# Reordering the opening of a graph-network kernel: who issues the loads, in which order, and which engine copies the first pair

## Chip, cores, metric

One core of one Trainium2 chip. The metric is the device time of one launch in microseconds (us).

## The reference, cut to what matters

For each of 64 graphs of 256 nodes and 256 channels: layer norm and ReLU; then a gated update fed by a convolution branch and a message branch.

```python
h  = relu(bn(conv1d(xc, conv1_w, pad=0)))            # 256 x 256, one tap
h  = bn(conv1d(h, conv2_w, pad=8))                   # 256 x 256 x 17 taps
x_conv = relu(h + xc).T
A   = exp(-dist) * mask;  msg = relu(x @ w_msg.T + b_msg)
x_nmp = A @ msg
# ... GRU gates from [x_conv, x_nmp] and x; the result is added to the input
```

All is float32. The 17-tap convolution is done as a short transform along the nodes with 47 products per block, so the filters must first be transformed too: this is work that only the start of the launch has.

## The kernel before

The kernel takes the graphs as 32 pairs, in eight blocks of four pairs. Before the first block it must (1) load x, normalize it, turn it with TensorE and run conv1 on four pairs; (2) load the filter taps (4.46 MB as `taps`, 119 rows of 7 input channels times 17 taps, loaded in three *thirds* for each half of the channels, `dc`), multiply them with three constant matrices (`points`, one for each *pass*), 57 *filter steps* of two matmuls each (four instructions in the trace), copy each result out on ScalarE and store it to DRAM (`filt`, 12.3 MB); (3) read `filt` back one kind at a time (`wb`) for the products.

```python
norm(0)                                  # pair 0 on VectorE
...
w_c1 = const.tile([P, DC, D], FP)
nc.scalar.dma_start(out=w_c1, ...)
s1, h1_shift = fold_bn(bn_vecs(bn1, "bn1", nc.scalar), "bn1")   # strided: one element per packet
...
def load_taps(dc, a, b, eng):
    eng.dma_start(out=taps[:, a:b, dc, :],
                  in_=c2_wT[dc * P + a * KG:dc * P + b * KG].rearrange("(g k) t o -> (k t) g o", k=KG))
...                                       # three loads of points, on nc.scalar
for h in range(3):
    for dc in range(DC):
        load_taps(dc, h * (NG - 1) // 3, (h + 1) * (NG - 1) // 3, nc.scalar if dc else nc.sync)
...
def transpose_h(i):                       # copies on ScalarE; x of pairs 2 and 3 loaded by ScalarE's queue
    ...
            nc.scalar.activation(HT[i][:, dc, :], p, AF.Relu)
    if i + 2 < B // G:
        load_x(i + 2, nc.scalar if i < 2 else nc.sync)
...
steps = [(m, g) for m in range(len(PASSES)) for g in range(NG)]
transpose_h(0); norm(1)
for j in range(PB):                       # PB = 4 pairs, four filter steps each
    if j > 0:
        transpose_h(j)
    if 0 < j < PB - 1:
        norm(j + 1)
    conv1(j)
    run(split_steps(j))
    for m, n in steps[j * 4:(j + 1) * 4]:
        filters(m, n, nc.sync)
forward()                                 # the block's transform, on VectorE
for j, (m, n) in enumerate(steps[PB * 4:]):          # the other 41 filter steps
    filters(m, n, nc.gpsimd if j % 2 else nc.sync)
```

`filters` writes PSUM with TensorE, copies on ScalarE into one of six staging tiles `fo`, and stores that. The queues run in order: ScalarE issues its loads among its own instructions. In the traces PE is TensorE and PEld its weight loads, DVE is VectorE, ACT ScalarE, POOL GpSimd and SP SyncE; a q behind a name (ACTq) marks the issue of a transfer.

Of the kernel before, what the change touches and what calls it, by code (L numbers as in the profile page):

```python
# [13 lines left out]
FP = mybir.dt.float32  # L14
U16 = mybir.dt.uint16
AF = mybir.ActivationFunctionType
ALU = mybir.AluOpType
# [284 lines left out]
def kernel(  # L302
# [26 lines left out]
    nc = tc.nc  # L329
    P = 128  # L330
    B, N, D = x.shape
    G = 2
    GB = 8
    PB = GB // G
    NB = B // GB
    DC = D // P
    MC = N // P
    W = G * N
    TAPS = c2_wT.shape[1]
    SE = se_wT.shape[1]  # L340
# [3 lines left out]
    NW = N // L  # L344
# [4 lines left out]
    const = ctx.enter_context(tc.tile_pool(name="const", bufs=1))  # L349
    work = ctx.enter_context(tc.tile_pool(name="work", bufs=1))  # L350
    stage_ctx = ExitStack()
    stage = stage_ctx.enter_context(tc.tile_pool(name="stage", bufs=1))
    psum = ctx.enter_context(tc.tile_pool(name="psum", bufs=1, space=bass.MemoryType.PSUM))
# [21 lines left out]
    def load_rows(t, src, i, eng):  # L375
        for g in range(G):
            eng.dma_start(out=row_tile(t, g), in_=rows(src, G * i + g))

    def load_x(i, eng=nc.sync):
        X[i] = work.tile([P, G * MC, D], FP, name="x", bufs=2)  # L380
        load_rows(X[i], x, i, eng)
# [23 lines left out]
    def load_adj(i, eng=nc.gpsimd):  # L405
        if i >= B // G:
            return
        if i < BY_DMA:
            ADJ[i] = work.tile([P, G * MC, N], FP, name="adj")
            load_rows(ADJ[i], adj, i, eng)  # L410
            return
        ADJH[i] = late.tile([P, 2 * MC, W], U16, name="adjh")
        for q in range(2 * MC):
            eng.dma_start(out=ADJH[i][:, q], in_=ADJD[i][:, q])
# [24 lines left out]
    ident = const.tile([P, P], FP)  # L439
    make_identity(nc, ident)  # L440
    neg_half = const.tile([P, G * MC], FP)
    nc.gpsimd.memset(neg_half, -0.5)

    pace = Pace()

    def mm(p, w, v, columns, **kw):
# [3 lines left out]
    def transpose(p, v):  # L450
        nc.tensor.transpose(p, v, ident)  # L451
        pace.tensor(P / 2)

    PSUM, ACT = 0.2, 0.9

    HT, MSG, E, AT, XNM = {}, {}, {}, {}, {}


    def norm_steps(i):
# [26 lines left out]
    def run(steps):  # L486
        for n, call in steps:
            pace.vector(n)
            call()

    def norm(i):
        a, b = norm_steps(i)
        run(a)
        pace.vector(0, pace.dve + 1.4)
        run(b)

    norm(0)

    def vec(src, name, eng=nc.gpsimd):
        k = src.shape[0] // P  # L500
        t = const.tile([P, k], FP, name=name)
        eng.dma_start(out=t, in_=src.rearrange("(k p) -> p k", p=P))
        return t

    def bn_vecs(params, name, eng=nc.gpsimd):
        return [vec(a, f"{name}_{s}", eng) for a, s in zip(params, "gbmv")]

    def fold_bn(params, name, factor=1.0):
        g, b, m, v = params
        scale = const.tile([P, DC], FP, name=f"{name}_scale")  # L510
        shift = const.tile([P, DC], FP, name=f"{name}_shift")
        nc.vector.tensor_scalar(scale, v, BN_EPS, None, ALU.add)
        nc.gpsimd.tensor_tensor(scale, scale, neg_half[:, :DC], ALU.pow)
        nc.vector.tensor_mul(scale, scale, g)
        nc.vector.tensor_mul(shift, m, scale)
        nc.vector.tensor_sub(shift, b, shift)
        if factor != 1.0:
            nc.vector.tensor_scalar(scale, scale, factor, None, ALU.mult)
        return scale, shift

    w_c1 = const.tile([P, DC, D], FP)
    nc.scalar.dma_start(out=w_c1, in_=c1_wT.rearrange("(k p) o -> p k o", p=P))
    s1, h1_shift = fold_bn(bn_vecs(bn1, "bn1", nc.scalar), "bn1")


    KG = P // TAPS
    NG = -(-P // KG)
    taps = stage.tile([KG * TAPS, NG, DC, D], FP, name="taps")

    def load_taps(dc, a, b, eng):  # L530
        eng.dma_start(out=taps[:, a:b, dc, :],
                      in_=c2_wT[dc * P + a * KG:dc * P + b * KG].rearrange("(g k) t o -> (k t) g o", k=KG))

    PASSES = [range(0, 6), range(6, 12), range(12, 16)]
    points = []
    for n, bins in enumerate(PASSES):
        f = filter_points(bins, TAPS)
        m = np.zeros((KG, TAPS, KG, f.shape[1]), np.float32)
        for k in range(KG):
            m[k, :, k] = f  # L540
        t = stage.tile([KG * TAPS, KG * f.shape[1]], FP, name=f"points{n}")
        nc.scalar.dma_start(out=t, in_=nc.inline_tensor(m.reshape(KG * TAPS, -1), name=f"points{n}").ap())
        points.append(t)
    for h in range(3):
        for dc in range(DC):
            load_taps(dc, h * (NG - 1) // 3, (h + 1) * (NG - 1) // 3, nc.scalar if dc else nc.sync)
    for dc in range(DC):
        last = c2_wT[dc * P + (NG - 1) * KG:(dc + 1) * P]
        nc.sync.dma_start(out=taps[:last.shape[0] * TAPS, NG - 1, dc, :], in_=last.rearrange("k t o -> (k t) o"))


    Z = const.tile([P, 1 + MC, G * MC, Q], FP, name="z")
# [5 lines left out]
    h1 = const.tile([P, G * DC, L, NW + 2], FP, name="h1")  # L558
# [3 lines left out]
    PT, Sv, T = (Slots(t, GB * DC, L // 4, NW) for t in (PTt, Svt, Tt))  # L562
    Yu = V

    def aux():
        return psum.tile([P, W], FP, name="aux", bufs=3)

    def acc():
        return psum.tile([P, W], FP, name="acc", bufs=5)


    def transpose_h(i):
        if i >= B // G:
            return
        HT[i] = work.tile([P, DC, W], FP, name="hT", bufs=6)
        for dc in range(DC):
            p = aux()
            for j in range(G * MC):
                transpose(chunk(p, j // MC, j % MC), X[i][:, j, dc * P:(dc + 1) * P])
            nc.scalar.activation(HT[i][:, dc, :], p, AF.Relu)  # L580
        if i + 2 < B // G:
            load_x(i + 2, nc.scalar if i < 2 else nc.sync)



    def conv1(i):
        if i >= B // G:
            return
        for o in range(DC):
            p = acc()  # L590
            for k in range(DC):
                mm(p, w_c1[:, k, o * P:(o + 1) * P], HT[i][:, k, :], W, start=(k == 0), stop=(k == DC - 1))
            nc.scalar.activation(h1.rearrange("p (g o) s b -> p o g s b", o=DC)[:, o, :, :, 1:1 + NW],  # L593
                                 p.rearrange("p (g s b) -> p g s b", g=G, b=NW),
                                 AF.Relu, bias=h1_shift[:, o:o + 1], scale=s1[:, o:o + 1])
        pace.vector(0, pace.pe + ACT)

    def split_steps(i):
# [15 lines left out]
    def filters(m, g, eng):  # L614

        kinds = filt[m].shape[1]
        size = min(KG, P - g * KG)
        p = acc()
        for dc in range(DC):
            mm(p[:size * kinds, dc * D:(dc + 1) * D], points[m][:size * TAPS, :size * kinds],  # L620
               taps[:size * TAPS, g, dc, :], D, start=True, stop=True)
        t = stage.tile([P, W], FP, name="fo", bufs=6)
        nc.scalar.copy(t[:size * kinds], p[:size * kinds])
        eng.dma_start(
            out=filt[m][g * KG:g * KG + size].rearrange("k t c o -> (k t) (c o)"), in_=t[:size * kinds])
# [219 lines left out]

    w_ih = const.tile([P, 2 * DC, 3 * D], FP)
    w_hh = const.tile([P, DC, 3 * D], FP)
    steps = [(m, g) for m in range(len(PASSES)) for g in range(NG)]
    transpose_h(0)
    norm(1)  # L850

    w_msg = const.tile([P, DC, D + SE], FP)
    nc.sync.dma_start(out=w_msg[:, :, :D], in_=msg_wT.rearrange("(k p) o -> p k o", p=P))
    nc.gpsimd.dma_start(out=w_msg[:, :, D:], in_=se_wT.rearrange("(k p) s -> p k s", p=P))
    b_msg = const.tile([P, D + SE], FP)
    for t, v in ((b_msg[:, :D], msg_b), (b_msg[:, D:], se_b)):
        nc.gpsimd.dma_start(out=t, in_=bass.AP(tensor=v.tensor, offset=v.offset, ap=[[0, P], [1, v.shape[0]]]))
    load_adj(0, nc.sync)
    bn2 = bn_vecs(bn2, "bn2")
    b_ih, b_hh = vec(ih_b, "b_ih"), vec(hh_b, "b_hh")  # L860
    for j in range(PB):
        if j > 0:
            transpose_h(j)
        if 0 < j < PB - 1:
            norm(j + 1)
        conv1(j)
        run(split_steps(j))
        for m, n in steps[j * 4:(j + 1) * 4]:
            filters(m, n, nc.sync)
    s2, h2_shift = fold_bn(bn2, "bn2", 1.0 / L)  # L870
    b_rz = const.tile([P, 2 * DC], FP)
    nc.vector.tensor_add(b_rz, b_ih[:, :2 * DC], b_hh[:, :2 * DC])
# [2 lines left out]
    forward()  # L875
    for j, (m, n) in enumerate(steps[PB * 4:]):
        filters(m, n, nc.gpsimd if j % 2 else nc.sync)
        if j + PB * 4 == 2 * NG - 10:
            for n in range(3):
                for kind in range(3):  # L880
                    load_kind(0, n, kind)
# [5 lines left out]
    for b in range(NB):  # L887
        i = b * PB
# [41 lines left out]
        stats, scale = norm_steps(nxt + 1)  # L930
# [33 lines left out]
        stats, scale = norm_steps(nxt + 2)  # L964
# [11 lines left out]
        stats, scale = norm_steps(nxt + 3)  # L976
# [70 lines left out]
```

## Time and profile before

| | before |
|---|---|
| time, median of 3 runs | 1899.43 us (1896.17 to 1899.59) |
| TensorE busy in the profiled run | 1827.6 of 1895.5 us |
| conv1 of pair 0 starts | 27.48 us |
| 16th filter step ends | 68.6 us |
| first message product (all filter steps done) | 111.51 us |
| first filter product | 115.12 us |

The last three are milestones read from TensorE's rows in the timeline. The message product stands right behind the last filter step in TensorE's order, so its start is the length of the opening. To read the rows of the waits: who waited, for whom, total us, times, longest. A row of the timeline has start, duration, engine, line, operation, out<-in, shapes and count, and in brackets the idle time before it and what ended that. A row of the windows has the window and its length, the busy time of PE, PEld, DVE, ACT and POOL, each with the number of instructions, then the granted clock, the DMA share and GB/s. The DMA share adds up the times of packets, which can overlap, so it can pass 1. The rows that the prediction rests on are shown in it.

### The profile page before, as it was taken

The page shows a single profiled execution, that of the slowest core. Times are in us where ns is not written, and L with a number is a line of the kernel's source. Part 1 is how long each engine was busy: PE and PEld are TensorE (multiplying, and loading weights), DVE is VectorE, ACT ScalarE, POOL GpSimd, SP SyncE. Part 2 cuts the span into 40 slices and gives each one's busy share as a digit, 9 for nine tenths or more (in the row PEclk, how much of TensorE's full clock was granted, in tenths as well). Part 3 has the DMA queues.
Part 4 walks back from the last instruction along what each step waited for, and adds up shares of the span by engine and source line. Part 5 has one row for each costly group of instructions (what it writes and reads, how often), then busy time and mean ns, then how long its engine had stood idle before and what let it go on. Part 6 is the DMA issues. An engine that isn't in the chain of part 4 may idle for free.

```text
span 1895.5 us, 21978 instructions
## 1 busy us (share of the span) xinstructions
PE 1827.6 (96%) x7708; PEld 1136.6 (60%) x7708; DVE 1393.1 (73%) x2667; ACT 639.4 (34%) x1338; POOL 208.2 (11%) x324
## 2 busy tenths in 40 slices
PE   3999999999999999999999999999999999999997
PEld 2677445865549554694458755495546944586543
DVE  2888648996499945998379964999559983798522
ACT  1534322243313443244232433134432352224311
POOL 2110110110111010111101001101101111010000
PEclk9999999999999999999999999999999999999999
DMA  5777331762318431482316613274313923073010
GB/s 161 253 237 216 91 87 36 195 176 57 85 48 244 107 93 52 112 239 56 89 34 191 182 54 82 54 237 114 90 55 106 239 62 78 23 186 104 2 43 23
DMA packets 180215, 217.63 MB, mean 115 GB/s; under 512 B 86146, under 2 KB 105858, under 8 KB 180105
## 3 DMA queue, kind: packets, MB, share of 16 engines
q1 hardware_dynamic: 145228, 156.03, 28.8%
q0 software_dynamic: 30432, 56.53, 12.7%
q10 hardware_dynamic: 4445, 3.67, 0.6%
q8 instruction: 61, 1.00, 0.2%
q14 instruction: 49, 0.40, 0.1%
HBM read 156.54 MB, written 44.30 MB: 106 GB/s over the span
## 4 chain that ended last, share of the span: by engine, by line
PE 82%; DVE 8%; DMA 4%; issue 3%; ACT 2%; POOL 1%; POOLq 0%; DVEq 0%; ACTq 0%
PE acc L447 70%; PE aux L447 8%; PE aux L451 3%; DMA taps<-in_c_wT_dram 1%; DVE Yv L59 1%; PE aux L736 1%; DVE e L743 1%; DVE Yv L62 1%; DMA x<-in_x_dram 1%; DVE T L65 1%; DVE Yv L65 1%; DVE V L65 1%; DMA wb<-filt 1%; DVE msg L708 1%; DVE T L62 0%
## 5 line engine op out<-in xcount | busy, mean ns | idle before, releaser
L447 PE MATMUL acc<-hT,w_hh 128*128 128x512 f32 x768 | 353.9, 597 | 1.9 <-ACT h L593 1.9
L447 PE MATMUL acc<-xnm,w_ih 128*128 128x512 f32 x768 | 353.0, 594 | 0.0
L447 PE MATMUL acc<-Yv,w_ih 128*128 128x512 f32 x768 | 341.1, 593 | 9.5 <-ACT Yv L696 9.5
L447 PEld LDWEIGHTS acc<-Yv,w_ih 128*128 128x128 f32 x768 | 145.2, 190 | 196.3 <-issue 177.2
L447 PEld LDWEIGHTS acc<-xnm,w_ih 128*128 128x128 f32 x768 | 145.6, 190 | 183.3 <-issue 181.3
L447 PEld LDWEIGHTS acc<-hT,w_hh 128*128 128x128 f32 x768 | 143.5, 191 | 169.5 <-issue 161.4
L797 ACT ACTIVATE tr<-acc,b_rz 128x512 f32<-128x512 f32 x64 | 44.0, 687 | 540.8 <-PE acc L447 540.8
L799 DVE SCALAR_TENSOR_TENSOR gn<-tr,gn 128x512 f32<-128x512 f32 x64 | 44.2, 690 | 207.7 <-ACT tr L797 207.7
L825 POOL DMA_DIRECT2D out_dram<-y x64 | 39.2, 617 | 886.4 <-DVE y L824 885.0
L447 PE MATMUL acc<-hT,w_c 128*128 128x512 f32 x256 | 117.9, 604 | 15.2 <-ACT hT L580 15.2
L447 PE MATMUL acc<-U,wb 128*128 128x128 f32 x1024 | 124.6, 276 | 0.5 <-DMA wb<-filt 0.5
L447 PE MATMUL acc<-V,wb 128*128 128x128 f32 x1024 | 124.8, 275 | 0.0
L447 PEld LDWEIGHTS acc<-U,wb 128*128 128x128 f32 x1024 | 120.5, 192 | 4.3 <-DVE Yv L59 2.3
L59 DVE SCALAR_TENSOR_TENSOR V<-T,V 128x256 f32<-128x256 f32 (+2 forms) x224 | 121.5, 606 | 0.3
L447 PEld LDWEIGHTS acc<-V,wb 128*128 128x128 f32 x1024 | 119.5, 192 | 0.0
L447 PE MATMUL aux<-e,msg 128*128 128x256 f32 x464 | 104.9, 379 | 0.0
L447 PEld LDWEIGHTS aux<-e,msg 128*128 128x128 f32 x464 | 86.1, 190 | 11.4 <-issue 1.0
L476 POOL TENSOR_TENSOR rstd<-rstd,neg_half 128x4 f32<-128x4 f32 x32 | 36.3, 1135 | 502.0 <-DVE rstd L475 502.0
L824 DVE TENSOR_TENSOR y<-aux,y 128x512 f32<-128x512 f32 x64 | 41.1, 683 | 68.4 <-PE aux L451 68.4
L447 PE MATMUL aux<-w_msg,hT 128*128 128x259 f32 x384 | 89.4, 381 | 0.0
L65 DVE TENSOR_TENSOR V<-h 128x512 f32<-128x512 f32 x64 | 43.8, 684 | 60.8 <-ACT h L593 60.8
L447 PEld LDWEIGHTS acc<-hT,w_c 128*128 128x128 f32 x256 | 49.2, 194 | 65.2 <-issue 45.1
(141 smaller groups left out, 2727.6 us busy)
## 6 DMA issues: line engine op xcount, KB each, us to landing
wb<-filt SPq DMA_DIRECT2D x376, 256.0 KB
y<-in_x_dram POOLq DMA_DIRECT2D x64, 256.0 KB, 5.7
out_dram<-y POOLq DMA_DIRECT2D x64, 256.0 KB, 5.1
x<-in_x_dram SPq DMA_DIRECT2D x60, 256.0 KB
halves_d<-halves SPq DMA_DIRECT2D x116, 128.0 KB
adjh<-halves_d POOLq DMA_DIRECT2D x116, 128.0 KB, 5.5
filt<-fo SPq DMA_DIRECT2D x26, 252.0 KB
filt<-fo POOLq DMA_DIRECT2D x10, 252.0 KB, 5.6
```

Of the source, the lines that this page charges most:

```text
L59: return self.step(out, lambda: self.v.scalar_tensor_tensor(out, x, s, y, op0=ALU.mult, op1=ALU.add))
L62: return self.step(out, lambda: self.v.tensor_add(out, x, y))
L65: return self.step(out, lambda: self.v.tensor_sub(out, x, y))
L447: nc.tensor.matmul(p, w, v, **kw)
L451: nc.tensor.transpose(p, v, ident)
L476: nc.gpsimd.tensor_tensor(t["rstd"], t["rstd"], neg_half, ALU.pow)
L708: nc.vector.tensor_add(MSG[i][:, g, c, :], p[:, :D + SE], b_msg)
L736: nc.tensor.matmul(p[:, :N], ZT[rows_q, :P], ZT[rows_q, P:], start=True, stop=True)
L797: nc.scalar.activation(tr, pr, AF.Tanh, bias=b_rz[:, dc:dc + 1], scale=0.5)
L799: nc.vector.scalar_tensor_tensor(gn, tr, 1.0, gn, op0=ALU.add, op1=ALU.mult)
L824: nc.vector.tensor_add(row_tile(Y[i], g), p, row_tile(Y[i], g))
L825: nc.gpsimd.dma_start(out=rows(out, G * i + g), in_=row_tile(Y[i], g))
```

## The change

Its intent: let nothing that TensorE needs early stand behind something that is needed late. Small vectors come as rows of 128 elements and are turned by TensorE; ScalarE issues only what is needed first, the rest goes to SyncE in order of need; filter steps of all three passes run on the first third of the taps; pair 0's two copies are VectorE's. Cut to its core:

```diff
+    load_vectors("bn1", bn1, nc.scalar)
+    w_c1 = const.tile([P, DC, D], FP)
+    nc.scalar.dma_start(out=w_c1, in_=c1_wT.rearrange("(k p) o -> p k o", p=P))
+    load_taps(0, *THIRDS[0], nc.sync)
+    load_taps(1, *THIRDS[0], nc.scalar)
...
+    bn1 = columns("bn1")                  # TensorE transpose, VectorE copy
+    nc.scalar.activation(const.tile([P, 1], FP, name="unused"), neg_half[:, :1], AF.Relu)
...                                        # the points stay here, on nc.scalar
-    for h in range(3):
-        for dc in range(DC):
-            load_taps(dc, h * (NG - 1) // 3, (h + 1) * (NG - 1) // 3, nc.scalar if dc else nc.sync)
+    load_taps(1, *THIRDS[1], nc.scalar)
...
-            nc.scalar.activation(HT[i][:, dc, :], p, AF.Relu)
+            if i == 0:
+                nc.vector.tensor_scalar(HT[i][:, dc, :], p, 0.0, None, ALU.max)
+            else:
+                nc.scalar.activation(HT[i][:, dc, :], p, AF.Relu)
...                                        # the same for h1 in conv1
-            load_x(i + 2, nc.scalar if i < 2 else nc.sync)
+            load_x(i + 2)
...
-    steps = [(m, g) for m in range(len(PASSES)) for g in range(NG)]
+    FIRST = THIRDS[0][1]
+    steps = [(m, g) for g in range(FIRST) for m in range(len(PASSES))]
+    steps += [(m, g) for m in range(len(PASSES)) for g in range(FIRST, NG)]
     transpose_h(0)
+    load_taps(0, *THIRDS[1], nc.sync)
     norm(1)
     for j in range(PB):
...
+        if j == 1:
+            for dc in range(DC):
+                load_taps(dc, *THIRDS[2], nc.sync)
+            for dc in range(DC):
+                load_last_taps(dc, nc.sync)
...                                        # w_msg, its bias, adj(0), bn2 rows: at j == 2
-        if j + PB * 4 == 2 * NG - 10:     # filt is first read after this step
+        if (m, n) == (1, NG - 4):
```

## The prediction

> **What bounds the kernel now.** I read the page first: its busy line, then its slices.
>
> ```profile
> span 1895.5 us, 21978 instructions
> ...
> PE 1827.6 (96%) x7708; PEld 1136.6 (60%) x7708; DVE 1393.1 (73%) x2667; ACT 639.4 (34%) x1338; POOL 208.2 (11%) x324
> ...
> PE   3999999999999999999999999999999999999997
> ```
>
> TensorE is busy 96% of the span; the idle share is 1895.5 − 1827.6 = 67.9 us. One slice is 47.4 us, and the first is the only one that stands at 3 tenths. The change touches nothing but the start, so its prize is TensorE's idle time there. Next I asked the view of waits for the first 150 us:
>
> ```profile
> ACT L580 <- DMA taps<-in_c_wT_dram: 25.5, 1, 25.5
> ...
> ACT fo L623 <- DMA filt<-fo: 18.3, 16, 4.1
> ...
> PE acc L447 <- ACT hT L580: 15.2, 3, 14.6
> ...
> PE aux L451 <- DVE x L479: 10.6, 1, 10.6
> ...
> PE acc L447 <- ACT fo L623: 5.7, 4, 3.2
> ...
> PE acc L447 <- ACT h L593: 4.0, 1, 4.0
> ```
>
> The four rows of PE sum to 15.2 + 10.6 + 5.7 + 4.0 = 35.5 us: this is all that the start can give. The first row names the cause of the largest: ScalarE did nothing for 25.5 us, and what ended it was a tap transfer. The timeline shows how:
>
> ```profile
> 9.02 16.48 ACTq L531 DMA_DIRECT2D taps<-in_c_wT_dram  x3
> ...
> 10.57 2.30 PE L451 MATMUL aux<-ident,x 128*128 128x128 f32 x8 [10.57 <-DVE x L479]
> ...
> 25.53 1.28 ACT L580 ACT_TABLE_LOAD   x1 [25.53 <-DMA taps<-in_c_wT_dram]
> 26.82 1.08 ACT L580 ACTIVATE hT<-aux 128x512 f32<-128x512 f32 x2
> ...
> 27.48 5.38 PE L447 MATMUL acc<-hT,w_c 128*128 128x512 f32 x8 [14.61 <-ACT hT L580]
> ...
> 35.84 2.64 ACTq L377 DMA_DIRECT2D x<-in_x_dram  x2
> ...
> 38.61 1.45 ACT L593 ACTIVATE h<-acc,bn_shift,bn_scale 128x512 f32<-128x512 f32 x2 [10.70 <-DMA taps<-in_c_wT_dram]
> ```
>
> The first pair's transposes end at 10.57 + 2.30 = 12.87, but the copy that follows stands behind ScalarE's own issue of three tap loads (9.02 + 16.48 = 25.5) and a table load, so TensorE stands until 27.48. Then ScalarE is held again: its x loads for pair 2 are issued only at 35.84, and the copy of conv1 runs at 38.61, which is the 4.0 us row. The last view is the table of windows for the filter transform's second half:
>
> ```profile
> 76.00:90.00 14.00, 14.00 (x65) 11.07 (x65) 13.97 (x28) 7.09 (x13) 3.73 (x7) 1.00 0.90 270
> 90.00:101.00 11.00, 5.19 (x21) 2.36 (x20) 10.90 (x13) 3.07 (x6) 1.05 (x2) 1.00 0.81 306
> 101.00:112.00 11.00, 11.00 (x50) 7.07 (x51) 4.81 (x8) 7.56 (x16) 3.69 (x7) 1.00 0.67 192
> ```
>
> The last two columns are the DMA share and GB/s. From 76 to 101 us the transfers are nearly full and TensorE, which runs up to 11 filter steps ahead (6 staging and 5 PSUM buffers), stands 5.8 us. The timeline ends the filter steps on TensorE at 111.5 us; there the first message product starts. From there on the order of work is that of before.
>
> **What the skill says.** (1) "DMA: Bandwidth & Descriptors", section "Why a DMA increments its semaphore by 16 and not by 1": a transfer runs on the largest number of engines up to 16 that divides the slowest dimension. A tap load has 7 × 17 = 119 rows, so 7 engines; a filter store of 126 rows gets 14; x with 128 rows gets 16. The trace agrees: with taps in flight (12 to 28 us) the DMA share is 0.56 at 156 GB/s, little above 7/16 = 0.44, whichever of the two queues they use. (2) The same page, "Issuing engines are not separate DMA queues": all queues use the same 16 engines, so moving loads from ScalarE to SyncE frees ScalarE and adds no bandwidth. The 156 GB/s on two queues agree. (3) The same page, "Rules for kernel authors": a load without contiguous last dimension becomes one descriptor per element. The DMA view of the first 36 us counts 1824 packets under 512 B in 5.58 MB. (4) "ScalarE: Activation LUTs", section "What ACT_TABLE_LOAD costs", has 1283 ns; the trace has 1.28 us.
>
> **The change, part by part.**
>
> *First pair on VectorE.* hT and h1 of pair 0 leave ScalarE. VectorE adds 2 copies of 128x512 (about 0.68 us each, from the trace's 128x512 VectorE rows) and 2 × 2 operations for h1 (2.6 us together at most). x arrives as before, so the transposes end near 13. VectorE runs the bn1 fold first (0.16 us operations around one 0.70 us POOL power: to about 13.3), so the copies end near 14.7 and conv1 starts at about 14.0 instead of 27.5: **13.5 us earlier**. VectorE then runs norm(1) (1.4 + 0.36 + 0.17 + a 1.2 us wait + 1.54 = 4.7 us) to 19.4, then h1 to 22, then four splits (2.5 us) to 24.5. The PSUM copy is thus no longer at 38.6, and the **4.0 us** stall goes.
>
> *Tap order and queues.* The first filter steps need only thirds 0 of both halves and the points. Two loads of 714 KB at about 156 GB/s are 9.2 us; beside x (1 MB on all 16 engines, 3 us on each) they land near 16 to 17, and conv1 keeps TensorE till about 19. So the first four filter steps are not held. Interleaving the three passes makes 18 steps possible on these thirds, where before any step past the sixth needed a later third.
>
> *Per pair,* TensorE then has 8 transposes (1.0), 8 conv1 matmuls (3.6 with the wait for hT about 4.6) and four filter steps (4 × 0.88 = 3.5): 9 us, the pace that the trace shows from 51 to 60. Pairs 1 to 3 start at 23.5 and end at 23.5 + 3 × 9 = 50.5. At half clock for some us (the 36 to 44 window had 0.61) and for one hold I add 2.5: 53. Before, this point was at 68.2 (64.5 + 4 × 0.9). **15 us earlier.**
>
> *The hold.* SyncE now issues third 2 and the last taps (1.5 MB, 9.5 us on 7 engines) ahead of the second pair's filter stores. I put those stores' landing at 44 us: on each low engine 131 KB of x, 16 of w_c1, 620 of taps and 125 of eight filter steps are about 0.9 MB, at 156/7 = 22 GB/s 41 us from 3 us on. With six staging buffers, the copies of steps 11 and 12 wait a few us; part of it is in the 2.5.
>
> *The other 41 filter steps* took 111.5 − 68.2 = 43.3 us before (41 × 0.87 = 35.7 of matmul and 5.8 of stalls on stores). Now they hold 8.4 MB of stores instead of 8.2, the same prefetch of 2.3 MB of filters (issued after step 40, not 28, among smaller stores). Fewer other loads remain, but all is crowded into less time. I take 38 to 43: filters end at 91 to 96, against 111.5.
>
> *Vectors as rows.* 14 strided loads of 4-byte elements (256 or 768 each) become rows of 512 B; two TensorE transposes and two small VectorE copies are added, under 1 us. ScalarE's issue of four of them (2.4 us) lay beside the x load and was hidden; POOL's (17.8 to 22.3) too. Worth about 0 to 0.5 us by itself.
>
> *Early table load:* 1.28 us, no longer ahead of the first copy, already counted in the 13.5.
>
> **Sum.** 111.5 − 93.5 = 18, plus half a us of small things, less half for the bn2 transposes: a gain of 18. No wait downstream takes it back in my view: odd FFT work on VectorE, which ended near 94.4, moves forward with pair 3's splits (68.4 to about 51).
>
> **Rivals.** (a) *The DMA becomes the bound.* By 118 us before, the DMA views' windows sum to 0.34 + 6.62 + 7.03 + 6.97 + 2.91 = 23.9 MB. At the 290 GB/s that 76 to 100 us reached, that is 82 us, but taps hold 7 engines for 28 us. Against it: shares stood at 0.4 to 0.6 until 44. For it: 76 to 101. If it rules, filters end at 100 and the gain is 11: 1888. (b) *The wait moves to SyncE:* stores behind third 2 stop ScalarE and so the hT copies of pairs 2 and 3. Then 3 to 6 us are lost: 1885 to 1888. (c) *VectorE becomes the start's bound:* if norm(1) ahead of h1 delays split(0) and norm(2), each pair waits; it has 14 us of work in pair 0 and under 6 in each later pair of 9, so I expect no more than 2 us. (d) *Stores hide everything better than thought,* and TensorE stands only for the first 13 us and 2 more: gain 35.5 − 15 = 20 to 22, 1878.
>
> **Range and chances.** 1899.4 − 18 = **1881.4 us**. Rival (d) and a little less half clock give the low end 1875; (a) with (b) the high end 1890. Two per cent are 38 us, more than the 35.5 that stand idle, so faster by 2% is nearly ruled out; slower would need the whole gain and 38 us more to be lost.
>
> **What would show it right or wrong.** In the timeline after: conv1's first matmul at about 14 (not 27); no ACT row released by taps; pair 3's last filter step near 53; the first message product near 93; PE rows of the waits summing to some 17 us in the first 120, with "DVE x" at about 10 among them. From the message product to the end both traces should take the same 1784 us within 2. Wrong if "ACT fo <- DMA filt" rises well over 18.3 with PE behind it, if the first filter steps wait for taps, or if the products start by waiting for filters not yet loaded.

## The result, and the profile after

The changed kernel took 1896.05 us (1893.43 to 1900.28, 4 runs) beside 1899.51 for the kernel before (now also 4 runs). The ratio is 0.9986, 95% interval 0.9963 to 1.0009: the same. Ratios here are the mean time of one kernel's runs over that of the other's of the same rounds, so not quite the ratio of the quoted medians. The prediction had 1881.4 and a range of 1875 to 1890. Of the 18 us that were predicted, 3 to 4 came by the medians, and the interval does not tell even these from nothing.

The profiled execution of the changed kernel was its slowest run, so ends of spans are not compared below; milestones are. The page of the kernel after:

```profile
span 1898.5 us, 21985 instructions
...
PE 1836.8 (97%) x7710; PEld 1141.9 (60%) x7710; DVE 1398.1 (74%) x2675; ACT 637.4 (34%) x1335; POOL 206.4 (11%) x324
...
PE   6899899999999999999999999999999999999997
```

The first slice went from 3 to 6 tenths, so the start did improve; but the second has lost its nine. TensorE's busy time *rose* by 9.2 us, for two more small matmuls of some 0.24 us each. The waits of the kernel after, in its first 150 us:

```profile
ACT fo L646 <- DMA filt<-fo: 21.3, 14, 5.2
...
PE acc L479 <- ACT hT L599: 5.5, 3, 4.9
PE acc L479 <- ACT fo L646: 5.0, 5, 1.7
PE acc L479 <- DMA points<-points: 4.7, 2, 4.0
```

The 15.2 us wait for ScalarE's hT copy has shrunk to 5.5 and the row "ACT L580 <- DMA taps" is gone, as meant. A new row has come, 4.7 us for the points, and ScalarE's wait for filter stores has grown from 18.3 to 21.3. The timeline of the kernel after tells where each stands:

```profile
13.43 5.58 PE L479 MATMUL acc<-hT,w_c 128*128 128x512 f32 x8 [0.92 <-DVE hT L597]
...
23.05 1.10 PE L479 MATMUL acc<-taps,points 119*126 119x256 f32 x4 [4.04 <-DMA points<-points]
...
34.15 3.80 SPq L451 DMA_DIRECT2D taps<-in_c_wT_dram  x2
...
37.99 6.07 SPq L456 DMA_DIRECT2D taps<-in_c_wT_dram  x2
...
44.16 1.92 SPq L647 DMA_DIRECT2D filt<-fo  x4
...
51.40 1.16 ACT L646 COPY fo<-acc 126x512 f32<-126x512 f32 x2 [5.21 <-DMA filt<-fo]
...
53.10 6.22 PE L479 MATMUL acc<-hT,w_c 128*128 128x512 f32 x8 [4.93 <-ACT hT L599]
...
107.29 5.55 PE L479 MATMUL aux<-w_msg,hT 128*128 128x259 f32 x12
...
113.61 1.05 PE L479 MATMUL acc<-Sv,wb 128*128 128x128 f32 x8
```

conv1 starts 14.0 us earlier. Then TensorE waits for the points; then the second pair's filter stores are issued only at 44.16, after the last taps, ScalarE finds no free staging tile for 5.21 us, and pair 3's conv1 stands. The message product comes 4.2 us earlier than before, the first filter product 1.5 us. The windows of the kernel after:

```profile
12.00:28.00 16.00, 10.40 (x23) 5.24 (x22) 12.09 (x37) 1.17 (x2) 3.73 (x7) 0.88 0.52 163
20.00:30.00 10.00, 6.31 (x16) 4.43 (x17) 6.44 (x19) 1.75 (x3) 1.01 (x1) 0.70 0.56 190
50.00:60.00 10.00, 6.89 (x12) 3.32 (x13) 0.00 (x0) 3.48 (x6) 0.00 (x0) 0.66 0.67 232
101.00:112.00 11.00, 9.28 (x23) 5.37 (x22) 1.88 (x5) 3.67 (x7) 2.07 (x4) 0.57 0.43 139
```

Each of the two waits is followed by a stretch of low granted clock, and so is the ragged end of the filter steps; in the last window before, the clock was 1.00. This accounts for most of the added busy time: up to the first filter product the mean clock was 0.89 against 0.97 before, and TensorE was busy for 87.5 against 79.4 us. The Trainium skill, page "TensorE: Matmul & The Clock Gate", section "HAM oscillation — how this bites in real kernels", describes it: after an idle gap of more than about 3.4 us the clock falls to half. The traces agree for the two waits: gaps of 4.04 and 4.93 us, then 0.70 and 0.66. They do not show that the gap must be that long: no gap at the ragged end is over 1.73 us, and in after_taps16 below the clock was 0.50 from 43.2 to 46.6 us, behind a gap of 1.74 us. Part of each of the two waits is paid a second time, as slower work after it.

Two causes are then possible. **Theory H**: the gain went into these holds and their clock; take the holds away and it comes back. **Rival B**: the transfers set the end of the filter steps, and waits on TensorE before it are only where the slack shows. In B's special form it is the taps, which by the skill's divisor rule run on 7 of 16 engines: the DMA share from 12 to 28 us is 0.52 at 163 GB/s, much as before the change (0.56 at 156).

### The profile page after: what moved, and what is told of

The parts are those of the page before. It is cut to its first block, busy times and chain, and to the rows that moved or that the text cites. A ratio compares the mean times of both kernels' runs of the same rounds, so it can differ in the third digit from the quotient of the medians.

```text
span 1898.5 us, 21985 instructions
## 1 busy us (share of the span) xinstructions
PE 1836.8 (97%) x7710; PEld 1141.9 (60%) x7710; DVE 1398.1 (74%) x2675; ACT 637.4 (34%) x1335; POOL 206.4 (11%) x324
## 4 chain that ended last, share of the span: by engine, by line
PE 82%; DVE 8%; DMA 4%; issue 3%; ACT 1%; POOL 1%; ACTq 0%; POOLq 0%; SPq 0%; DVEq 0%
PE acc L479 70%; PE aux L479 8%; PE aux L483 3%; DVE Yv L59 1%; PE aux L759 1%; DMA taps<-in_c_wT_dram 1%; DVE e L766 1%; DVE Yv L62 1%; DVE T L65 1%; DVE Yv L65 1%; DMA wb<-filt 1%; DMA x<-in_x_dram 1%; DMA filt<-fo 1%; DVE msg L731 1%; DVE V L65 1%
## 5 line engine op out<-in xcount | busy, mean ns | idle before, releaser
L479 PEld LDWEIGHTS aux<-e,msg 128*128 128x128 f32 x464 | 86.2, 191 | 11.3 <-issue 1.0
L847 DVE TENSOR_TENSOR y<-aux,y 128x512 f32<-128x512 f32 x64 | 41.1, 684 | 68.4 <-PE aux L483 68.4
```

Source lines behind the costliest of these rows:

```text
L479: nc.tensor.matmul(p, w, v, **kw)
L847: nc.vector.tensor_add(row_tile(Y[i], g), p, row_tile(Y[i], g))
```

## The experiments

All gave right results. All timed runs were in the fast state (before_again, a single look, has none told), each beside the kernel before, and the ratio is to that of the same rounds. "Message" is the start of the first message product in the profiled run. That is one execution for each row: for both_taps16 and best it was the fastest of the timed runs; for third2_late, both_moves, half_taps16 and after_taps16 one between; for the others, but the two of before, the slowest.

| run | built on | 16th step ends | message | median us | ratio to before |
|---|---|---|---|---|---|
| before | | 68.6 | 111.5 | 1899.43 | |
| before_again | before | 68.2 | 110.7 | 1897.81 (1 run) | |
| rows_only | before | 68.4 | 110.8 | 1898.92 | 0.9998 |
| vector_only | before | 70.2 | 114.3 | 1899.57 | 0.9999 |
| before_taps16 | before | 64.1 | 108.9 | 1893.79 | 0.9972 |
| after | | 62.8 | 107.3 | 1896.05 | 0.9986 |
| points_first | after | 64.0 | 107.0 | 1896.84 | 0.9990 |
| third2_late | after | 54.6 | 107.1 | 1897.66 | 0.9998 |
| both_moves | after | 55.5 | 108.1 | 1898.64 | 1.0000 |
| third2_scalar | after | 56.3 | 104.8 | 1897.29 | 0.9983 |
| half_taps16 | both_moves | 49.4 | 100.2 | 1890.67 | 0.9955 |
| both_taps16 | both_moves | 48.5 | 95.1 | 1888.68 | 0.9954 |
| taps16_stores16 | both_taps16 | 49.6 | 104.4 | 1894.35 | 0.9963 |
| after_taps16 | after | 52.0 | 97.6 | 1888.09 | 0.9935 |
| points_taps16 | after | 52.7 | 98.0 | 1886.72 | 0.9919 |
| best | after | 49.0 | 91.6 | 1882.51 | 0.9911 |

The 95% intervals are 0.0014 to 0.0023 wide to either side. No ratio is faster by 2%. Those of rows_only, vector_only, after, points_first, third2_late and both_moves are not clear of 1, and third2_scalar's only just (0.9969 to 0.9998).

### points_first, third2_late, both_moves: take the holds away

```diff
 # points_first: the three loads of points, moved ahead of these two
+    ...nc.scalar.dma_start(out=t, in_=nc.inline_tensor(...))   # x3
     load_taps(0, *THIRDS[0], nc.sync)
     load_taps(1, *THIRDS[0], nc.scalar)
 # third2_late: out of the head of pair 1, behind the stores of pairs 1 and 2
-        if j == 1:
-            for dc in range(DC):
-                load_taps(dc, *THIRDS[2], nc.sync)
-            for dc in range(DC):
-                load_last_taps(dc, nc.sync)
...
         for m, n in steps[j * 4:(j + 1) * 4]:
             filters(m, n, nc.sync)
+        if j in (1, 2):
+            load_taps(j - 1, *THIRDS[2], nc.sync)
+            load_last_taps(j - 1, nc.sync)
 # both_moves: both
```

> Edit: the three loads of the filter points are issued on ScalarE's queue ahead of the tap loads, not behind them. Theory H (gain lost to holds of TensorE and the half clock that follows each): the 4.04 + 0.64 us waits for the points and the half-clock stretch at 24 us go; the 16th filter step ends near 56 instead of 62.8, the first message product near 102 instead of 107.3, time 5 us under the changed kernel's 1896. Rival B (the transfers set the end of the filter steps): the 16th step moves, but the first message product stays within 2 us of 107, time 1895 to 1897.

> Edit: the last third of the taps is issued one half after the second and one after the third pair's filter stores, not both ahead of the second pair's. Theory H: the 4.93 us wait at 48 us and the half clock after it go; 16th filter step near 56, first message product near 101 to 103, time 4 to 6 us under 1896. Rival B: the wait goes but the message product stays within 2 us of 107, time within 2 us of 1896.

> Edit: both of the above. Theory H: 16th step near 51, message product near 95, no half clock between 30 and 95 us, time near 1884. Rival B: 16th step near 51, yet the message product at 103 or later, the waits of ScalarE's copies for filter stores grow from 21 us to 28 or more, time 1890 or more.

The message product did not move: 107.0, 107.1 and 108.1 against 107.3, although with third 2 late the 16th step ended 7 to 8 us earlier. With the points first, TensorE waited for the taps instead (3.2 us), so there that hold was not removed but renamed, and pair 3's wait grew from 4.93 to 7.27 us. This is the timeline of both_moves:

```profile
24.14 6.32 PE L489 MATMUL acc<-taps,points 119*126 119x256 f32 x14 [4.98 <-DMA taps<-in_c_wT_dram]
...
68.98 29.86 PE L489 MATMUL acc<-taps,points 119*126 119x256 f32 x120 [7.04 <-ACT fo L646]
...
108.13 4.90 PE L489 MATMUL aux<-w_msg,hT 128*128 128x259 f32 x12
```

The wait of 4.0 us came back as one of 4.98 us for the taps, that of 4.93 us as one of 7.04 us behind the stores. This is rival B's outcome, with two misses in its own expectation: ScalarE's wait for stores came to 23.7 us, not 28, and the 16th step to 55.5, not 51. Theory H falls for the hold that was taken away, third 2's. The first hold was never taken away alone; but the message product stood at 107 to 108 us for 16th steps from 54.6 to 64.0, so an earlier start of the other steps brought nothing here.

### both_taps16 and half_taps16: spread the taps

```diff
     def load_taps(dc, a, b, eng):
-        eng.dma_start(out=taps[:, a:b, dc, :],
-                      in_=c2_wT[dc * P + a * KG:dc * P + b * KG].rearrange("(g k) t o -> (k t) g o", k=KG))
+        src = c2_wT[dc * P + a * KG:dc * P + b * KG].rearrange("(g k) t o -> (k t) g o", k=KG)
+        for lo, hi in ((0, 112), (112, KG * TAPS)):      # half_taps16: only for dc == 1
+            eng.dma_start(out=taps[lo:hi, a:b, dc, :], in_=src[lo:hi])
```

> Edit: both of the above, and each tap load of 119 rows is cut in one of 112 rows (16 engines by the divisor rule) and one of 7. Theory H: taps were hidden by then, so within 2 us of the run with both moves. Rival B: engines 0 to 6 carried 4.4 MB of taps in 28 us; spread, they free some 15 us of these engines for stores, and the message product comes 4 to 8 us earlier than with both moves alone.

> Edit: the kernel with both moves, but only the taps of the second channel half are cut in 112 and 7 rows. A dose: with none cut the first message product was at 108.1, with both at 95.1. Theory B (seven engines' time): about half way, 100 to 104. If it is one particular load that mattered (the first third, that the first steps wait for, or the last, that stores wait behind), it lies near one of the ends.

Same bytes, six more transfers, and the message product comes 13.0 us earlier, more than the 4 to 8 expected; the medians of the same rounds differ by 10.0 us. With half of the loads cut the message product comes 7.9 us earlier, a little over half of the way. The times confirm that the cut helps (0.9955 and 0.9954 with intervals clear of 1), but do not tell half from whole; the dose is read from one trace each. Nor is either part of it half way: the 16th step came 6.1 of 7.0 us earlier, the 41 steps after it took 52.6, 50.8 and 46.6 us. So the dose says less than its sum. The window from 12 to 28 us, of both_moves and then of both_taps16:

```profile
12.00:28.00 16.00, 10.11 (x22) 5.45 (x21) 12.75 (x39) 1.17 (x2) 3.76 (x7) 0.86 0.51 179
...
12.00:28.00 16.00, 14.79 (x44) 7.99 (x43) 12.65 (x39) 5.45 (x9) 3.89 (x7) 1.00 0.82 232
```

TensorE is busy 14.79 of 16 us, where both_moves had 10.11. The clock of 1.00 is not to be taken at its word there: the clock's record begins at 18.7 us, and conv1, from 13.60, took 6.22 us, pair 1's 3.70.

### before_again, before_taps16, after_taps16, taps16_stores16

```diff
 # before_again: no edit
 # before_taps16: the cut of load_taps above, in the kernel before; after_taps16: the same, in the changed one
 # taps16_stores16: both_taps16 and
-        eng.dma_start(
-            out=filt[m][g * KG:g * KG + size].rearrange("k t c o -> (k t) (c o)"), in_=t[:size * kinds])
+        dst = filt[m][g * KG:g * KG + size].rearrange("k t c o -> (k t) (c o)")
+        even = size * kinds // 16 * 16
+        for lo, hi in ((0, even), (even, size * kinds)):
+            eng.dma_start(out=dst[lo:hi], in_=t[lo:hi])
```

> The kernel before, unchanged, for a second trace. It tells whether the stretch from the first filter product to the end (1780.4 us in the first trace, 1783 to 1785 in the changed kernels' five) and the stall near 233 us (1.95 us against 3.3 to 5.0) belong to the kernel or to the execution. If to the execution: a stall of 2 to 5 us again anywhere in that range and 1780 to 1785; if to the kernel: 1.9 to 2.1 and 1780 to 1781.

The second trace of the kernel before has the message product 0.8 us earlier, so differences of a us in milestones mean nothing. The stretch after the first filter product took 1781.7 us, and the stall near 233 us was 3.0 us. That stretch took 1780 to 1787 us in all sixteen traces; the two of before are at its low end, but so is the fastest kernel (1781.0). I put it down to the execution, without proof.

> Edit: the kernel before with nothing of the change, but each tap load cut in 112 rows on 16 engines and 7 rows on 7. Rival B (seven engines' traffic set the end): ScalarE is free of its tap loads some 10 us earlier, conv1 starts near 18 to 20 instead of 27.5, the first message product falls from 111.5 to 98 to 103, time 8 to 12 us under before, with none of the change. Theory H: the start moves but the message product does not come before 107.

A miss for B as I had put it: the message product came to 108.9, not to 98 to 103, and the time fell by 0.3%. ScalarE is still held: in this kernel it issues all thirds of its half of the taps ahead of its first copy, which comes at 23.4 us. So in the order of the kernel before, spreading the taps is worth little alone; ScalarE's queue holds the start. The 16th step came 4.5 us earlier, and the 41 steps after it took 44.8 us instead of 42.9.

> Edit: the changed kernel with the tap loads cut so, points and third 2 left in their places. Rival B: first message product near 95 to 98, time 8 to 11 us under before, the two moves add nothing. Theory H: without the moves the waits at 19 and 48 us stay, and the message product is 6 us or more behind the run with both moves and the cut (95.1).

As B expected, without either move: 97.6 us and 11 us under before. The cut alone gave 0.28%, the change alone 0.14%, both together 0.65%. By the traces each uncovers the other's limit: with the taps cut, the change brings the message product forward by 11.3 us (108.9 to 97.6) instead of 4.2, and the median by 5.7 us instead of 3.5; the times alone, with intervals of 0.15 to 0.23%, do not show that the two together are worth more than their sum. The cut also took away the wait for the points and left 1.74 us of pair 3's 4.93: the 16th step came 10.8 us earlier than in the changed kernel, and the 41 steps after it took 45.6 us instead of 44.5. So this pair of kernels does not tell B from H. The pair both_moves and both_taps16 does better: there the 41 steps became 6.0 us shorter.

> Edit: both moves and the cut taps, and each filter store cut too: 112 and 14 rows of 126, 64 and 13 of 77, so that 14 engines become 16 for most of it. Rival B in its strong form (the busiest engines still pace the stores): 12 MB over 16 instead of 14 engines saves up to 6 us, the message product near 89 to 93. If the stores are paced by something else (the issue of twice the transfers, landing time, the writes themselves), it stays at 94 to 97 or gets later.

The message product came 9 us later than in both_taps16, and ScalarE waited 31.7 us for stores. From 76 to 90 us the DMA share and rate fell, both_taps16 first:

```profile
76.00:90.00 14.00, 12.00 (x54) 7.39 (x52) 10.28 (x11) 5.43 (x10) 2.68 (x6) 1.00 0.95 306
...
76.00:90.00 14.00, 12.95 (x57) 8.97 (x56) 11.33 (x12) 7.36 (x14) 7.27 (x15) 1.00 0.79 237
```

The two traces are the slowest run of one kernel and the fastest of the other, and the ratios (0.9963 and 0.9954) do not tell them apart. So the cut of the stores did not help, rival B's strong form is a miss, and by the traces twice as many transfers, half of them small, cost more than the spread gave. Whether issue or landing costs it was not separated.

### rows_only and vector_only: parts of the change alone

```diff
 # rows_only, on the kernel before: bn_vecs and vec replaced by
+    load_vectors("bn1", bn1, nc.scalar)
+    s1, h1_shift = fold_bn(columns("bn1"), "bn1")
...
+    load_vectors("bn2", bn2 + [ih_b, hh_b], nc.gpsimd)
...
+    *bn2, b_ih, b_hh = columns("bn2")
 # vector_only, on the kernel before: the two "if i == 0" of the change
```

> Edit: the kernel before with the vectors as rows and TensorE turns alone. Both theories: the strided loads lay beside other work, so first message product within 2 us of 111.5 and time within 3 us of before. If the small packets had clogged the transfers' engines, conv1 would start 2 us or more before 27.3.

As expected, nothing: 110.8 us and a ratio of 0.9998.

> Edit: the kernel before with the first pair's copies on VectorE alone; ScalarE still issues its tap loads and the x of pairs 2 and 3. Theory B (the end of the filter steps is set by the taps on seven engines and the stores after them): conv1 starts at 13 to 14 instead of 27.3 and yet the first message product stays at 106 to 111, time 0 to 5 us under before. Theory H: the 14 us wait is gone and nothing new holds TensorE as in the changed kernel, so the message product comes near 100.

conv1 started at 13.82 as both theories had it, but the message product came to 114.3, later than either said; the time was the same (0.9999). The timeline of vector_only has the reason:

```profile
9.26 15.95 ACTq L531 DMA_DIRECT2D taps<-in_c_wT_dram  x3
...
25.34 9.88 ACTq L377 DMA_DIRECT2D x<-in_x_dram  x2
...
35.25 1.28 ACT L630 ACT_TABLE_LOAD   x1 [35.25 <-issue]
...
39.15 5.55 PE L447 MATMUL acc<-hT,w_c 128*128 128x512 f32 x8 [8.71 <-ACT hT L583]
```

ScalarE goes from its tap loads into the issue of pair 2's x, which takes 9.88 us, and is free at 35.25; pair 1's conv1 waits 8.71 us. Earlier work on one engine only brought forward the next user of a held queue. Why that issue took so long was not tested; taps still in flight are my guess.

### third2_scalar and points_taps16, best: what was still open

```diff
 # third2_scalar: points_first and
-                load_taps(dc, *THIRDS[2], nc.sync)
+                load_taps(dc, *THIRDS[2], nc.scalar)
 # points_taps16: after, points first, taps cut
 # best: points_taps16 and
-        t = stage.tile([P, W], FP, name="fo", bufs=6)
+        t = stage.tile([P, W], FP, name="fo", bufs=7)
```

> Edit: the changed kernel with the points first, and the last third of the taps issued from ScalarE's queue at the same place, so that it isn't ahead of the filter stores in their own queue. Order theory (stores wait because they stand behind the taps in SyncE's queue): the 7.3 us wait before pair 3's conv1 goes and the first message product comes to 100 or earlier. Engine theory (the taps fill seven of the engines that every store needs, whatever the queue): the wait stays or turns up elsewhere, message product at 104 to 109, time 1893 to 1899.

The wait before pair 3's conv1 went, which both readings allowed, and TensorE waited elsewhere: 4.8 us for the first taps, 1.88 at 63 us, 3.16 at 96. The message product came to 104.8, near the early end of the engine theory's 104 to 109. So taking third 2 out of the stores' queue bought 2 us of message product against points_first (107.0); spreading the taps on the same kernel (points_taps16) bought 9. It is mostly how the taps occupy the transfer engines, not the order in one queue. No view names the engine of a packet, but the packed traces have each packet's times. In before, from 14 to 28 us, 7 or 8 packets of 1 KB (the taps') were under way at once for 11.0 of 14 us, on both queues together, and ScalarE's queue alone never had more than 7. In before_taps16, from 14 to 22 us, it was 16 to 19 for 5.5 of 8 us. So the taps of both queues shared some seven engines, and with the cut some sixteen. That the stores need the same engines is argued and not shown: if the divisor rule gives a store 14 of 16, at least five of any seven are among them.

> Edit: the changed kernel with the cut tap loads, the points first and a seventh staging buffer. Theory B: the transfers still pace the second half at 250 to 260 GB/s, so the message product at 94 to 97 and 1885 to 1889 us. If buffers, not transfers, limited the stores' pace, the message product at 92 or earlier.

> Edit: the fastest kernel so far with six staging buffers again, that is the changed kernel with cut taps and the points first. If the seventh buffer gave the gain from 97.6 to 91.6 of the first message product: 96 to 98 here, time 1886 to 1888. If the points' place did: 91 to 93, time 1882 to 1884.

best took 1882.51 us (1879.7 to 1883.54), 0.9911 of before with an interval of 0.9895 to 0.9927: the fastest of all. Its message product at 91.6 us is not theory B's 94 to 97 but the other outcome, "92 or earlier", in which buffers limit the pace of the stores; the rate from 76 to 90 us was 316 GB/s, as in after_taps16, and not the 250 to 260 expected. That would mean that once the taps are spread the transfers alone no longer set the end. points_taps16 with six tiles had 98.0, just as after_taps16 (97.6): the traces point to the seventh staging tile, not the points' place. They do not prove it: best's trace is its fastest run and points_taps16's its slowest, and of the 6.4 us between them 1.1 is there when conv1 starts (13.17 and 14.30), before any staging tile is used. The times cannot tell either (points_taps16 spread from 1880.1 to 1892.9, and the intervals of the two ratios overlap). A seventh tile without the cut was not run, so what it would give in the changed kernel is open. An eighth tile does not fit: it asked for 55.31 KB per partition where 55.22 were left. The timeline of best:

```profile
91.60 4.58 PE L490 MATMUL aux<-w_msg,hT 128*128 128x259 f32 x12
...
96.89 1.05 PE L490 MATMUL acc<-Sv,wb 128*128 128x128 f32 x8
```

## Why the prediction was wrong

**What bounds the kernel, and the prize: right.** Nothing but the start changed, and two per cent was out of reach: the best of all versions gained 0.9%.

**First pair on VectorE: right.** conv1 started at 13.43, predicted about 14.0; h1's second relu ended at 20.6, predicted 22; the splits at 23.2, predicted 24.5. The early table load stood at 5.60, out of the way, and the vectors as rows did nothing (rows_only), as told; there are ten such loads, not the 14 that I counted. The 68.2 that I had for the 16th step before is 68.6 by TensorE's rows; I had counted from the weight load at 64.5, not the matmul at 64.94.

**"So the first four filter steps are not held": wrong.** I checked the taps and forgot that the points stand behind a tap load in ScalarE's queue. TensorE stood 4.7 us. The step "they land near 16 to 17" holds at best for two loads on an empty machine: in points_first, where the points went ahead, TensorE waited for taps till 23.21.

**"At half clock for some us and for one hold I add 2.5: 53": mis-sized.** The 16th step ended at 62.8. In place of 2.5 us stood the points' 4.7, pair 3's 4.9, and two low-clock stretches.

**"The other 41 filter steps ... 38 to 43": mis-sized, 44.5, and not the right term.** third2_late and both_moves brought the 16th step to 54.6 and 55.5, almost the predicted 53, and these steps then took over 52 us. Their length was not a property of the steps: it was what the transfers left. A small slip besides: the stores left after 16 steps are 8.7 MB, not 8.4 (11 steps of 252 KB and 5 of 154 KB are done by then).

**Where the 16.5 us went.** I predicted the first filter product at 93.5 + 3.6 = 97.1 us; it came at 113.6. The parts: 62.8 − 53 = 9.8 in the first 16 steps, 44.5 − 40.5 = 4.0 in the others, and 6.3 − 3.6 = 2.7 in the message product, which ran in the low-clock window.

**The step that failed** is the setting aside of rival (a), the DMA as the bound, and with it the 38 to 43 us for the other 41 steps: "At the 290 GB/s that 76 to 100 us reached, that is 82 us, but taps hold 7 engines for 28 us." I had both facts and did not add them. What the runs showed in its place: with third 2's hold taken away the message product stayed at 107.1 us, and with the taps spread in the same order it came from 108.1 to 95.1. Transfers that fill the same seven engines come one after another there: 28 us of taps; 12.3 MB of stores at some 250 GB/s (the 76 to 90 window of third2_late has 249), 49 us; 2.3 MB of filters read back and some 4 MB of other loads at 290, 22 us; 3 us until the first packet. That is 102 us, an estimate from the traces' numbers, against a last filter step at 107. It is rough: it puts every store and load on those seven engines evenly with the others, and the traces do not show the load of one engine. Instead I added the seven engines' time only up to 44 us, for one hold, and costed the rest stage by stage as if it began on free engines. Before, the taps came first and the stores after them (the first store was issued at 45.05 us). The change starts the stores beside the taps, and where both need the same engines that is no gain.

**Its own signs** said so. ScalarE's wait for filter stores rose from 18.3 to 21.3 us with TensorE behind it; the first filter steps waited, though for points; TensorE's waits in the first 120 us summed to 26, not 17. From the message product to the end the trace took 1791.2 us where 1784 within 2 was forecast (1784.0 and 1785.3 in the two traces of before): 2.7 of it is the slower message product, the rest lies in the spread of the stretch after it that before_again left open.

**The rivals.** (b), the wait that moves to SyncE, did happen (4.93 us), but removing it gave nothing. (c), VectorE, did not. (d), 1878, came in no run; best is nearest.

**The mechanism of the gain was right once the taps were spread.** best has the 16th step at 49.0 (predicted 53), the message product at 91.6 (93.5) and 1882.5 us (1881.4). That it comes so near is partly luck: it has a seventh staging tile and the points first, of which the prediction knew nothing. The changed kernel with the cut alone (after_taps16) has 52.0, 97.6 and 1888.1.

## What to carry to other kernels

Before predicting a reordering, add up the time of each transfer engine over the whole stage, with the number of engines that each transfer's shape lets it use; if that sum is near the stage's length, reordering moves only the waits. Removing a wait and seeing the milestone stand still is the sign that the wait was slack. Fix the transfer's shape first (112 + 7 rows instead of 119): with that, the same reordering brought its milestone forward by 11.3 us instead of 4.2, in one trace each.

## What the Trainium skill lacked or had wrong

- "DMA: Bandwidth & Descriptors", section "Why a DMA increments its semaphore by 16 and not by 1": the divisor rule held up for the taps. Cutting 119 rows in 112 and 7 raised the DMA share from 0.51 to 0.82 and the rate from 179 to 232 GB/s (both_moves and both_taps16, 12 to 28 us). The page does not say how much such a cut is worth beside other traffic: 13.0 us of a 108 us stage in one trace each, 10.0 us of the medians.
- The same page, section "Rules for kernel authors", has "Use all 16 engines", and warns in another row that transfers under 64 KB are mostly overhead; it does not weigh the two. Cutting the stores (54 of 57 have 126 or 77 rows, by the rule 14 or 11 engines, which no run here shows) left small pieces of 28 and 26 KB, and in the traces the stage was 9 us longer. The small pieces of the taps, 42 KB each, came with a gain.
- The same section says that strided elements should be made contiguous. It gives no hint of when that is worth nothing: ten such loads of 1 and 3 KB, turned into rows, left the time as it was (ratio 0.9998 ± 0.0015).
- The same page, section "Issuing engines are not separate DMA queues", calls the sequencer's time to issue a DMA usually small beside the DMA itself. Here ScalarE's issue of three loads of 714 KB took 16.48 us before, when all taps were under way for some 28, and of two of 256 KB 9.88 us in vector_only, and its own copies stood behind them.
- "TensorE: Matmul & The Clock Gate", section "HAM oscillation — how this bites in real kernels": its gap of about 3.4 us fits two of the three low stretches here, as told above, but not the third, nor the one in after_taps16 behind 1.74 us (shorter idles are the subject of the section after it). It has the cost in a whole kernel; here, up to the first filter product, TensorE's busy time rose by 8.1 us.
